# A four-layer graph network: layer 1's message and update products as 2x2 blocks over pairs of graphs

## The chip, the core and the metric

The kernel runs on one core of one Trainium2 chip. The metric is the time of one execution on the device in microseconds (us); lower is better. The engines are called here as in the profile: PE (TensorE, matrix products; PEld is its weight load), DVE (VectorE), ACT (ScalarE), POOL (GpSimd) and SP (SyncE, which only issues DMAs here).

## What is computed

There are 128 graphs of 128 nodes, with 256 features a node, and an integer adjacency matrix for each graph. Four layers follow one another, each inside a residual connection and a layer norm. All numbers are float32.

```
def _L1_gnn_ref(x, adj, W_msg, W_upd, bias):
    a = adj.astype(x.dtype)
    h = jnp.einsum('bnf,fu->bnu', x, W_msg)
    msg_sum = jnp.einsum('bij,biu->bju', a, h)
    deg = jnp.sum(a, axis=1)
    messages = jnp.where(deg[..., None] > 0, msg_sum / jnp.maximum(deg, 1.0)[..., None], 0.0)
    out = jnp.einsum('bnf,fu->bnu', x, W_upd) + messages + bias
    return jax.nn.relu(out)

x = _layernorm(x + _L0_gnn_ref(x, adj, a0, a1, a2, a3), axis=-1)   # four scores by edge type, softmax
x = _layernorm(x + _L1_gnn_ref(x, adj, W_msg, W_upd, bias), axis=-1)
x = _layernorm(x + _L2_gnn_ref(x, adj, weight, w_ih, ...), axis=-1)  # three steps of a gated unit (GRU)
x = _layernorm(x + _L3_gnn_ref(x, adj, W, a), axis=-1)             # attention
```

The change is in layer 1: the two products x W_upd and x W_msg, each 128 nodes x 256 features by 256 x 256, for every graph.

## The kernel before

**Groups.** Four graphs make a group (G = 4), and 32 groups pass through the four layers. The 256 features lie as two chunks of 128 (KC = 2)[...]. The work of several groups is interleaved: while one group is in its GRU, which takes two periods, others are in layers 0, 1 and 3.

**The order.** No engine order is written out by hand. The program first records all operations (`Op`), with what each must wait for, and gives each a nominal time with `paced(start, end)`: the layer's window in units of PERIOD, shifted by the group's number. Then a list scheduler at the end of the file issues them. It keeps for each engine the time at which it becomes free, with assumed costs (`pe_cost`, `dve_cost`, `act_cost`, `pool_cost`), an assumed DMA landing time (LANDING) and assumed hops between engines (HOP and PE_HOP for operations marked urgent, SLACK for the others). Among the operations that are ready by then it takes the one with the least nominal time. The GRU's operations are marked urgent; on all engines but PE they count as EAGER us earlier. The operations that copy an unfinished sum out of PSUM (`snapshot`) count as RUSH us earlier still. The scheduler also hands out buffers, PSUM banks among them. Every engine then runs its list strictly in the order so found, and waits where an operand is not there yet. Operations of POOL and DVE that the program takes to exclude one another are marked with `waits` and `holds`. All recorded calls are issued from one helper, so that every row of the profile has line L232, and rows are told apart by tile names.

**Layer 1** (`layer1`, from line 591). `s.x1T`, written `xT` there, holds the normalised output of layer 0 with features on partitions, [128, graph, chunk, node]. It comes by DMA; for group 0 by transposes on PE and a copy on ACT. `w_um` [128, chunk, 512] holds W_upd in its first 256 columns and W_msg in the rest. For each graph, lines 599 to 607 take a PSUM bank (`bank()`, tag `ps`, four of them; the GRU gates have four more, tag `gate`), add two products of 512 columns into it, one for each chunk, then copy the message half with ACT and add the bias to the update half with DVE, both into `hu`. Column 512 of `hu` is one, so that the product with the adjacency (line 611) gives the degree too. DVE divides, adds, takes the maximum with zero and adds the residual; `normalise` follows, and the result `xb` goes to the GRU.

**The GRU's gates** (`gru`, `sums`, `gate`) already form their products as 2x2 blocks with seven products. Blocks of features and of weights are added and subtracted first (`t_h` by POOL, `t_m` by DVE). Four of the products then accumulate in a bank called `shared`, which is copied out between them, and three go to the bank `other`.

**Layer 3** ends with `ninv`, the negated reciprocal of the softmax sums, four numbers a partition, made by DVE in line 876.

**Transposes** (`turned`, `back`): DVE transposes 32x32 blocks into a tile `z` (four buffers), SP writes it to DRAM and reads it back in block order.

Of the kernel before, what the change touches and what calls it, by code (L numbers as in the profile page):

```python
# [18 lines left out]
def kernel(  # L19
# [39 lines left out]
    B, N, D = x.shape  # L59
# [80 lines left out]
    def bank(tag="ps"):  # L140
        return tile_of(tag, [P, 512], 4, F32, psum)
# [94 lines left out]

    LANDING = 4.2
    HOP = 0.235  # L240
    PE_HOP = 0.55
    SLACK = 0.873

    def pe_cost(op, n, sums):
        return 0.11 if op == "transpose" else 0.222 if n <= P else 0.003 + n / 599.0
# [1 line left out]
    SPLIT = 0.056  # L247

    def dve_cost(op, n, sums):
        return 0.14 + n * (0.00056 if op in FAST else 0.00106)  # L250

    def act_cost(op, n, sums):
        return 0.6 if op == "dma_start" else 0.17 + n * 0.001 + (0.2 if sums else 0.0)
# [9 lines left out]
    engines = (PE, DVE, ACT, POOL, SP)  # L263


    PERIOD = 82.744
    SPAN = 2.0
    EAGER, RUSH = 5.34, 0.516
    L0_START, L0_END, L1_START, L1_END, L3_START, L3_END = -2.032, -1.293, -0.75, -0.05, 0.173, 0.919
    H_END, M_START, M_END = 0.179, 0.179, 0.503  # L270

    def paced(start, end, pe_only=False):

# [18 lines left out]
    neg_half = tile_of("neg_half", [P, G])  # L292
    acol = tile_of("acol", [P, 4, KC])
    w_um = tile_of("w_um", [P, KC, 2 * D])
    bias_row = tile_of("bias_row", [P, D])
    bih = tile_of("bih", [P, NGC])
    bhh = tile_of("bhh", [P, NGC])
# [10 lines left out]
    def weights():  # L308
# [91 lines left out]
        DVE.tensor_add(brz, bih[:, : 2 * KC], bhh[:, : 2 * KC])  # L400
        DVE.tensor_scalar_mul(brz, brz, 0.5)
        DVE.tensor_scalar_mul(bhn, bhh[:, 2 * KC :], 0.5)

        scr = tile_of("t_n", [P, D], 2)
        for c in range(KC):
# [16 lines left out]
    def turned(src, n, tag):  # L422

        way = tile_of(f"way_{tag}", [n, P, P], 8 if tag == "2" else 4, F32, dram)
        for first in range(0, n, G):
            z = tile_of("z", [P, G, P], 4)[:, : min(n, G)]
            DVE.transpose(z, src[:, first : first + G])
            SP.dma_start(out=way[first : first + G].rearrange("n p c -> p n c"), in_=z)
        return way
# [161 lines left out]
    def layer1(g, s):  # L591
        x1, a_f, xT = s.x1, s.a_f, s.x1T

        s.m_gt = tile_of("m_gt", [P, G, N], 3, U8)
        POOL.tensor_scalar(s.m_gt, a_f, 0.0, None, op0=OP.is_gt)
        s.a_ne = tile_of("a_ne", [P, G, N], 3, BF16)
        DVE.tensor_scalar(s.a_ne, a_f, 0.0, None, op0=OP.not_equal)
        hu = []
        for b in range(G):
            hu.append(tile_of("hu", [P, 2 * D + 1], 2))  # L600
            POOL.memset(hu[b][:, 2 * D :], 1.0)
            ps = bank()
            with PE:
                for c in range(KC):
                    PE.matmul(ps, xT[:, b, c, :], w_um[:, c, :], start=(c == 0), stop=(c == KC - 1))
            ACT.copy(hu[b][:, D : 2 * D], ps[:, D:])
            DVE.tensor_add(hu[b][:, :D], ps[:, :D], bias_row)
        res = tile_of("xb", [P, G, D], 2)
        for b in range(G):
            ps = bank()  # L610
            PE.matmul(ps[:, : D + 1], a_f[:, b, :], hu[b][:, D:], start=True, stop=True)
            fac = tile_of("fac", [P, 1], 4)
            DVE.tensor_scalar_max(fac, ps[:, D : D + 1], 1.0)
            DVE.reciprocal(fac, fac)
            DVE.scalar_tensor_tensor(
                fac, ps[:, D : D + 1], 0.0, fac, op0=OP.is_gt, op1=OP.mult
            )
            DVE.scalar_tensor_tensor(
                res[:, b, :], ps[:, :D], fac, hu[b][:, :D], op0=OP.mult, op1=OP.add
            )  # L620
            if b % 2 == 1:
                two = slice(b - 1, b + 1)
                DVE.scalar_tensor_tensor(res[:, two], res[:, two], 0.0, x1[:, two], op0=OP.max, op1=OP.add)
        normalise(res, *statistics(res, "1"), "1", g == 0)

        s.way_x2 = tile_of("way_x2", [P, G, D], 4, F32, dram)
        SP.dma_start(out=s.way_x2, in_=res)
        s.hT, s.parts, s.ways = [], [], []
        for c in range(KC):
            t = tile_of("h0T", [P, T], 4)  # L630
            cols = slice(c * P, (c + 1) * P)
            if g == 0:
                turned_quick(t, [res[:, b, cols] for b in range(G)])
            s.ways.append(turned(res[:, :, cols], G, "2"))
            if g > 0:
                back(t, s.ways[c])
            s.hT.append(t)
        for c in range(KC):
            s.parts.append(split(res[:, :, c * P : (c + 1) * P], POOL))
# [171 lines left out]
    def layer3(g, s, first, last):  # L811


        n = last - first
        end = g == NG - 1
        names = LAST if first else {}
        two, three = ("2b", "3b") if first else ("2", "3")

        def tile(tag, shape, bufs=1):
            tag, bufs = names.get(tag, (tag, bufs))  # L820
            return tile_of(tag, shape, bufs)

        rT = []
        for c in range(KC):
            t = tile("rT", [P, n * N], 2)
            cols = slice(first * N, last * N)
            back(t, s.ways[c][first:last])
            (DVE if end else POOL).tensor_add(t, t, s.hT[c][:, cols])
            rT.append(t)
        x3 = tile("xc", [P, n, D])  # L830
        SP.dma_start(out=x3, in_=s.way_x2[:, first:last])
        for c in range(KC):
            cols = slice(c * P, (c + 1) * P)
            DVE.tensor_add(x3[:, :, cols], x3[:, :, cols], s.hn[c][:, first:last])
        mv, rstd = statistics(x3, two)
        wh = tile("wh", [P, n, 2 + D])
        for b in range(n):
            ps = bank()
            with PE:
                for c in range(KC):  # L840
                    PE.matmul(
                        ps[:, : 2 + D], rT[c][:, b * N : (b + 1) * N], w3x[:, c, :],
                        start=(c == 0), stop=(c == KC - 1),
                    )
            ACT.mul(wh[:, b, :], ps[:, : 2 + D], rstd[:, b : b + 1])


        f = tile("e", [P, 4 * n, 32])
        e = f.rearrange("p (k b) c -> p b k c", [P, n, 4, 32], b=n)
        if end:  # L850
            ps = bank()
            with PE:
                for b in range(n):
                    PE.transpose(ps[:, b * N : (b + 1) * N], wh[:, b, 1:2].to_broadcast([P, N]), ident)
            rows = [ps[:, b * N : (b + 1) * N].rearrange("p (k c) -> p k c", c=32) for b in range(n)]
        else:
            z = tile_of("z_f", [P, 32])
            DVE.transpose(z, wh[:, :, 1:9])
            way = tile_of("way_f", [P, 32], 4, F32, dram)
            SP.dma_start(out=way, in_=z)  # L860
            SP.dma_start(out=f, in_=way.rearrange("(m r) c -> r m c", [8, 16, 32], r=8)[0].partition_broadcast(P))
            rows = [e[:, b] for b in range(n)]
        alpha = tile("alpha3", [P, n, N])
        POOL.memset(alpha, NEG3)
        for b in range(n):
            leaky(e[:, b], rows[b], wh[:, b, 0:1])
        BLOCKS = "p b (k c) -> p b k c"
        DVE.copy_predicated(
            alpha.rearrange(BLOCKS, c=32), s.m_gt[:, first:last].rearrange(BLOCKS, c=32), e
        )  # L870
        pT, rinv = softmax(alpha, three, end, tile)
        normalise(x3, mv, rstd, two, end)

        res = tile("xd", [P, n, D])
        ninv = tile_of(f"ninv_{three}", [P, n], 2)
        DVE.tensor_scalar_mul(ninv, rinv, -1.0)
        for h in range(n // 2):
            ps = bank()
            with PE:
                for j in range(2):  # L880
                    b = 2 * h + j
                    PE.matmul(ps[:, j * D : (j + 1) * D], pT[:, b, :], wh[:, b, 2:], start=True, stop=True)
            for j in range(2):
                b = 2 * h + j
                pb = ps[:, j * D : (j + 1) * D]
                ACT.activation(res[:, b, :], pb, AF.Relu, scale=rinv[:, b : b + 1])
                ACT.activation(pb, pb, AF.Relu, scale=ninv[:, b : b + 1])
            half = slice(2 * h, 2 * h + 2)
            ACT.activation(ps, ps, AF.Exp, scale=-1.0)
            (DVE if end else POOL).tensor_add(res[:, half], res[:, half], x3[:, half])  # L890
            DVE.scalar_tensor_tensor(
                res[:, half], ps.rearrange("p (b d) -> p b d", [P, 2, D], b=2), -1.0, res[:, half],
                op0=OP.add, op1=OP.add,
            )
        normalise(res, *statistics(res, three), three, end)
        SP.dma_start(out=out[g * G + first : g * G + last].rearrange("b n d -> n b d"), in_=res)
# [139 lines left out]
```

## Time and profile before

| | |
|---|---|
| median of 3 runs | 2764.72 us (2764.5 to 2765.69) |
| the profiled execution | 2763.69 us |
| its span, first to last instruction | 2761.8 us |
| mean granted TensorE clock | 0.991 |
| DMA | 321.88 MB, mean 117 GB/s |
| ACT copy hu<-ps, 128x256 | 128 times, mean 368 ns |
| DVE add hu<-ps,bias_row, 128x256 | 128 times, mean 413 ns |
| DVE t_z<-gate,t_z, 128x512 | 96 times, mean 668 ns |
| POOL t_h sums, 128x256 | 384 in four rows, together 323.7 us |
| DVE ninv<-rinv, 128x4 | 31 times, mean 676 ns |

A row of the profile names the engine, the operation, output<-inputs by tile name, the shape and the count; then the busy time in us and the mean of one in ns; then how long the engine was idle just before such instructions, and what ended that. A float32 product leaves two records, so that 512 records of 128x512 on `w_um` are 256 products: 8 for each of 32 groups. The ends of matmuls are modelled and overlap the next start.

### The profile page before, as it was taken

The numbers are of one execution on the slowest core, as the hardware profiler recorded it, in microseconds if no ns is written. First come the engines' busy times: TensorE is split into PE (matmuls) and PEld (weight loads), VectorE is DVE, ScalarE is ACT, GpSimd is POOL, SyncE is SP. The second block draws the span as 40 slices with busy tenths as digits, with TensorE's granted clock in tenths as the row PEclk, the third lists the DMA queues.
The fourth block names the chain that finished last, engine by engine and source line by source line (L and its number), as shares of the span: only waits on it lengthen the run. The fifth ranks groups of instructions, "written<-read, shape, count | busy, mean of one in ns | idle before, by whom it ended". The sixth has DMA issues, their size and how long they took to land.

```text
span 2761.8 us, 44048 instructions
## 1 busy us (share of the span) xinstructions
PE 2702.3 (98%) x13756; PEld 2138.1 (77%) x13756; DVE 2304.1 (83%) x5108; ACT 1584.2 (57%) x3704; POOL 1666.2 (60%) x1606
## 2 busy tenths in 40 slices
PE   8899999999999999999999999999999999999996
PEld 5677787887887887887887887887887887787774
DVE  5787888888888888888888888888888898888875
ACT  4454665555665655665655665655665655665554
POOL 4544666655666655666655666655676655675542
PEclk9999999999999999999999999999999999999996
DMA  5545555555555556555655556655556555545441
GB/s 121 129 90 99 115 126 129 120 109 124 122 125 131 121 108 129 118 124 133 121 107 127 121 121 134 121 110 123 121 121 134 124 109 120 116 110 118 99 88 43
DMA packets 1397130, 321.88 MB, mean 117 GB/s; under 512 B 1142560, under 2 KB 1388448, under 8 KB 1396896
## 3 DMA queue, kind: packets, MB, share of 16 engines
q1 hardware_dynamic: 1394448, 316.69, 53.7%
q10 hardware_dynamic: 2448, 2.36, 0.3%
q8 instruction: 111, 1.82, 0.3%
q14 instruction: 123, 1.01, 0.1%
HBM read 185.74 MB, written 133.15 MB: 115 GB/s over the span
## 4 chain that ended last, share of the span: by engine, by line
PE 94%; DVE 3%; POOL 1%; ACT 1%; DMA 1%; issue 1%; ACTq 0%; POOLq 0%; DVEq 0%; SPq 0%
PE gate L232 52%; PE ps L232 42%; DVE t_r L232 0%; POOL t_h L232 0%; DVE xb L232 0%; DVE st L232 0%; DMA rest<-in_L_gnn_w_hh_dram 0%; DVE z L232 0%; POOL rstd L232 0%; DMA hn<-in_L_gnn_weight_dram 0%; POOL xa L232 0%; DVE xa L232 0%; DVE t_d L232 0%; POOL t_d L232 0%; DVE hT L232 0%
## 5 line engine op out<-in xcount | busy, mean ns | idle before, releaser
L232 ACT ACTIVATE q<-gate,bhn 128x256 f32<-128x256 f32 x384 | 183.0, 477 | 314.4 <-PE gate L232 313.1
L232 PE MATMUL ps<-agT,c_gi 128*128 128x512 f32 x768 | 356.0, 592 | 0.0
L232 PE MATMUL gate<-t_h,w_hhT 128*128 128x256 f32 x1152 | 345.2, 381 | 5.7 <-ACT t_z L232 4.3
L232 PE MATMUL gate<-t_h,w_sh 128*128 128x256 f32 x1152 | 337.1, 383 | 4.2 <-ACT q L232 1.7
L232 POOL TENSOR_TENSOR rstd<-rstd,neg_half 128x4 f32<-128x4 f32 (+1 forms) x128 | 142.4, 1112 | 218.2 <-DVE rstd L232 215.1
L232 PEld LDWEIGHTS gate<-t_h,w_sh 128*128 128x128 f32 x1152 | 213.7, 191 | 62.8 <-issue 30.4
L232 PEld LDWEIGHTS ps<-xs,xT 128*128 128x128 f32 x2048 | 249.7, 193 | 11.5 <-ACT xs L232 2.6
L232 PEld LDWEIGHTS gate<-t_h,w_hhT 128*128 128x128 f32 x1152 | 211.7, 191 | 56.1 <-issue 16.3
L232 PE MATMUL ps<-xs,xT 128*128 128x128 f32 x2048 | 251.8, 276 | 2.2 <-ACT xs L232 1.3
L232 ACT COPY t_z<-gate 128x256 f32<-128x256 f32 x288 | 107.1, 372 | 244.6 <-PE gate L232 244.0
L232 PE MATMUL ps<-w_um,x1T 128*128 128x512 f32 x512 | 237.1, 595 | 0.2 <-ACT x1T L232 0.2
L232 PEld LDWEIGHTS ps<-agT,c_gi 128*128 128x128 f32 x768 | 145.8, 190 | 114.5 <-issue 106.0
L232 PE MATMUL gate<-agT,c_gi 128*128 128x256 f32 x768 | 229.2, 380 | 2.6 <-ACT agT L232 2.6
L232 PE MATMUL gate<-t_m,c_gi 128*128 128x256 f32 x768 | 228.5, 379 | 0.0
L232 PE MATMUL gate<-t_m,w_sm 128*128 128x256 f32 x768 | 228.4, 379 | 0.0
L232 PE MATMUL gate<-hT,w_hhT 128*128 128x256 f32 x768 | 222.8, 385 | 5.6 <-DVE hT L232 5.6
L232 POOL TENSOR_SCALAR mk<-a_f 128x512 uint8<-128x512 f32 x128 | 201.3, 1579 | 12.2 <-DVE alpha L232 6.6
L232 ACT ACTIVATE xs<-xT,acol 128x512 f32<-128x512 f32 x256 | 182.1, 717 | 40.9 <-PE ps L232 31.5
L232 POOL MEMSET hu<- 128x1 f32 x128 | 10.3, 96 | 303.8 <-DVE fac L232 224.5
L232 DVE TENSOR_TENSOR t_z<-gate,t_z 128x256 f32<-128x256 f32 x192 | 104.2, 543 | 101.4 <-ACT t_z L232 53.7
L232 POOL TENSOR_TENSOR t_d<-h0T,t_n 128x512 f32<-128x512 f32 x64 | 82.9, 1295 | 174.0 <-ACT t_n L232 171.1
L232 PEld LDWEIGHTS gate<-hT,w_hhT 128*128 128x128 f32 x768 | 141.8, 191 | 48.1 <-issue 23.6
(197 smaller groups left out, 7280.1 us busy)
## 6 DMA issues: line engine op xcount, KB each, us to landing
way_h<-z SPq DMA_DIRECT2D x190, 256.0 KB, 2.4
hn<-way_h SPq DMA_DIRECT2D x760, 64.0 KB, 2.4
way<-z SPq DMA_DIRECT2D x126, 256.0 KB, 3.2
x_blocks<-in_x_dram SPq DMA_DIRECT2D x256, 64.0 KB, 2.3
x_in<-in_x_dram SPq DMA_DIRECT2D x32, 512.0 KB, 3.8
way_x<-xb SPq DMA_DIRECT2D x32, 512.0 KB, 2.9
way_p<-z SPq DMA_DIRECT2D x62, 256.0 KB, 2.6
probT<-way_p SPq DMA_DIRECT2D x248, 64.0 KB, 2.3
```

The lines of the kernel that those rows point to most:

```text
L232: getattr(self.engine, name)(*[a.real() if isinstance(a, View) else a for a in args], **{k: a.real() if isinstance(a, View) else a for k, ...
```

## The change

Graphs are taken in pairs. Of a pair, x11 and x12 are the two feature chunks of the first graph, x21 and x22 those of the second; of the weights, b11 and b12 are chunk 0 of W_upd and W_msg, b21 and b22 chunk 1. The four 128x256 blocks of results (two graphs, two weights) are now formed from seven products of 256 columns instead of four of 512. Three sums of weights (`w_x`) and the difference that replaces b12 in `w_um` are made once, on POOL. Three sums of features for each pair (`t_x`) and the difference that replaces x21 in `xT` are made by POOL for both pairs of a group at a time. Each pair holds two banks; between the products in `shared` there is one bias addition by DVE and two copies by ACT. Further, `ninv` moves to ACT, `z` has three buffers, and constants of the scheduler have other values.

```diff
-    LANDING = 4.2
+    LANDING = 3.91
     HOP = 0.235
-    PE_HOP = 0.55
-    SLACK = 0.873
+    PE_HOP = 0.478
+    SLACK = 0.61
...
     def dve_cost(op, n, sums):
-        return 0.14 + n * (0.00056 if op in FAST else 0.00106)
+        return 0.095 + n * (0.00056 if op in FAST else 0.00106) + (0.08 if sums else 0.0)
...
-    PERIOD = 82.744
+    PERIOD = 88.831
     SPAN = 2.0
-    EAGER, RUSH = 5.34, 0.516
-    L0_START, L0_END, L1_START, L1_END, L3_START, L3_END = -2.032, -1.293, -0.75, -0.05, 0.173, 0.919
-    H_END, M_START, M_END = 0.179, 0.179, 0.503
+    EAGER, RUSH = 26.109, 4.31
+    L0_START, L0_END, L1_START, L1_END, L3_START, L3_END = -2.032, -1.293, -0.701, -0.122, 0.297, 0.767
+    H_END, M_START, M_END = 0.141, 0.122, 0.7
...
+    w_x = tile_of("w_x", [P, 3, D])
...
+        b11, b12, b21, b22 = [w_um[:, c, n * D : (n + 1) * D] for c in range(KC) for n in range(2)]
+        POOL.tensor_sub(w_x[:, 1], b22, b12)
+        POOL.tensor_sub(b12, b12, b11)
+        POOL.tensor_sub(w_x[:, 0], b22, b12)
+        POOL.tensor_sub(w_x[:, 2], b21, w_x[:, 0])
...
-            z = tile_of("z", [P, G, P], 4)[:, : min(n, G)]
+            z = tile_of("z", [P, G, P], 3)[:, : min(n, G)]
...
+        t = tile_of("t_x", [P, 3, 2, N])
+        x11, x12, x21, x22 = [
+            xT.rearrange("p (h j) c n -> p j c h n", [P, 2, KC, 2, N], j=2)[:, j, c] for j in range(2) for c in range(KC)
+        ]
+        POOL.tensor_add(t[:, 0], x21, x22)
+        POOL.tensor_sub(x21, x11, x21)
+        POOL.tensor_sub(t[:, 1], t[:, 0], x11)
+        POOL.tensor_sub(t[:, 2], x12, t[:, 1])
+        U, M = slice(0, D), slice(D, 2 * D)
         hu = []
-        for b in range(G):
-            hu.append(tile_of("hu", [P, 2 * D + 1], 2))
-            POOL.memset(hu[b][:, 2 * D :], 1.0)
-            ps = bank()
-            with PE:
-                for c in range(KC):
-                    PE.matmul(ps, xT[:, b, c, :], w_um[:, c, :], start=(c == 0), stop=(c == KC - 1))
-            ACT.copy(hu[b][:, D : 2 * D], ps[:, D:])
-            DVE.tensor_add(hu[b][:, :D], ps[:, :D], bias_row)
+        for h in range(G // 2):
+            pair = tile_of("hu", [P, 2, 2 * D + 1], 2)
+            POOL.memset(pair[:, :, 2 * D :], 1.0)
+            hu += [pair[:, 0], pair[:, 1]]
+            shared, other = bank(), bank()
+            first, second = 2 * h, 2 * h + 1
+
+            def add(cols, x, w, start=False, stop=False):
+                PE.matmul(cols, x, w, start=start, stop=stop, skip_group_check=True)
+
+            def snapshot(to):
+                ACT.copy(to, shared[:, :D])
+                ops[-1].rush = RUSH
+
+            add(shared[:, :D], xT[:, first, 0, :], w_um[:, 0, U], True)
+            DVE.tensor_add(pair[:, 0, U], shared[:, :D], bias_row)
+            add(other[:, U], xT[:, first, 1, :], w_um[:, 1, U], True)
+            add(shared[:, :D], t[:, 1, h], w_x[:, 0])
+            snapshot(pair[:, 0, M])
+            add(other[:, M], t[:, 0, h], w_um[:, 0, M])
+            add(shared[:, :D], xT[:, second, 0, :], w_x[:, 1])
+            snapshot(pair[:, 1, M])
+            DVE.tensor_add(pair[:, 1, M], other[:, M], pair[:, 1, M])
+            add(shared[:, :D], xT[:, second, 1, :], w_x[:, 2], stop=True)
+            DVE.tensor_add(pair[:, 1, U], shared[:, :D], bias_row)
+            add(other[:, M], t[:, 2, h], w_um[:, 1, M], stop=True)
+            DVE.tensor_add(pair[:, 0, : 2 * D], other, pair[:, 0, : 2 * D])
...
-        DVE.tensor_scalar_mul(ninv, rinv, -1.0)
+        ACT.mul(ninv, rinv, -1.0)
```

## The prediction

> **What bounds the kernel now.** I read the page's header and busy table first, then its costliest groups, then busy time by stretches of the span, then the waits of TensorE in the middle stretch, then the order in time. From the page:
>
> ```profile
> span 2761.8 us, 44048 instructions
> PE 2702.3 (98%) x13756; PEld 2138.1 (77%) x13756; DVE 2304.1 (83%) x5108; ACT 1584.2 (57%) x3704; POOL 1666.2 (60%) x1606
> ...
> PE 94%; DVE 3%; POOL 1%; ACT 1%; DMA 1%; issue 1%; ACTq 0%; POOLq 0%; DVEq 0%; SPq 0%
> ...
> L232 PE MATMUL ps<-w_um,x1T 128*128 128x512 f32 x512 | 237.1, 595 | 0.2 <-ACT x1T L232 0.2
> ```
>
> TensorE is busy 98% and makes up 94% of the chain that ended last. The last row is the group that the change replaces. The stretches (columns: length, then PE, weight loads, DVE, ACT, POOL) say where the idle 59 us lie:
>
> ```profile
> 0.00:270.00 270.00, 247.99 (x1254) 189.09 (x1255) 192.81 (x437) 125.44 (x282) 130.58 (x143) 0.99 0.52 110
> 270.00:2580.00 2310.00, 2307.17 (x11852) 1839.18 (x11851) 1989.71 (x4411) 1364.58 (x3196) 1457.53 (x1392) 1.00 0.56 120
> 2580.00:2761.80 181.80, 147.16 (x653) 109.86 (x651) 121.56 (x263) 94.17 (x228) 78.08 (x72) 0.88 0.35 78
> ```
>
> In the middle 2310 us TensorE is idle for 3; the rest is start (22) and drain (35). All that TensorE waited for in the middle is this:
>
> ```profile
> PE gate L232 <- ACT agT L232: 1.7, 1, 1.7
> PE gate L232 <- ACT t_z L232: 1.0, 2, 0.6
> ```
>
> So in the middle time is TensorE work, and only TensorE work counts. Busy time hides small gaps, because matmuls overlap in the records. The pitch from start to start, in the timeline, is the true price:
>
> ```profile
> 1000.55 1.88 PE L232 MATMUL ps<-w_um,x1T 128*128 128x512 f32 x4
> ...
> 1006.31 0.59 PE L232 MATMUL gate<-t_h,w_hhT 128*128 128x256 f32 x2
> 1006.74 0.59 PE L232 MATMUL gate<-hT,w_sh 128*128 128x256 f32 x2
> ```
>
> A float32 product is two records. Four records of 512 columns take 1.88 us, the last one 0.59 with its modelled end: (1.88 - 0.59) / 3 = 0.43 us a record, 0.86 a product. A product of 256 columns starts 0.43 after the one before it. Between 1000 and 1160 us I added up such pitches: 155.9 of 159.3 us, so some 2% are gaps that the busy row does not show, 49 us over the middle.
>
> **What the Trainium skill says.** "Perfetto Trace Analysis", section Identifying the Most-Contended Engine: busy time of matmuls is a poor measure, since they are pipelined. The trace agrees: mean record 595 ns, pitch 430. "FP8 and Floating Point Precision", TensorE Precision Notes: true FP32 takes four passes; the trace shows two records a product and a cost proportional to columns (0.86 for 512, 0.43 for 256), all that I use. "TensorE: Matmul & The Clock Gate", Weight-path perf modes: the fast weight load is not for FP32. Here a float32 load takes 190 ns and a bfloat16 one 99. This matters because halving the columns leaves a 190 ns load only 215 ns to hide behind; the 256-column gate products above keep exactly 0.43, so it still hides. "SBUF — State Buffer", Who interferes with whom: a VectorE instruction with two inputs in SBUF, or in a two-port mode, excludes a GpSimd one that reads SBUF for a whole instruction. The trace agrees: the 4-element ninv takes
>
> ```profile
> L232 DVE TENSOR_SCALAR ninv<-rinv x32: 176/665/989, 283.1 to 2750.5; 128x4 f32<-128x4 f32 x31, 128x2 f32<-128x2 f32 x1
> ```
>
> (minimum, median, maximum ns): 0.18 alone, 0.67 with a wait.
>
> **The change part by part.**
>
> *TensorE.* Removed: 8 products of 512 columns a group, 8 x 0.86 = 6.88 us. Added: 2 pairs x 7 products of 256 columns, 14 x 0.43 = 6.02. Saved 0.86 a group, 32 x 0.86 = 27.5 us, nearly all of it in the dense stretch (group 0 lies in the start). Loads rise by 12 records of 0.19, hidden as above.
>
> *Waits inside a pair.* The bank `shared` is read between its four products: one bias add (VectorE) and two snapshots (ScalarE), so three waits a pair, 192 in all, each with one product of 0.43 on `other` between. The GRU gates do the same (3 gates x about 3 waits x 96 steps, some 900). Lower bound 0, if other groups' products are issued in between. Upper bound on what such waits cost a dense stretch: if all 49 unseen us were theirs, 49 / 900 = 0.054 each, 192 x 0.054 = 10 us. I take 4. What one costs with nothing between is on the chain of the drain (start, length):
>
> ```profile
> 2693.78 1.24 PE gate L232 x2
> 2695.02 0.03 issue
> 2695.04 0.48 ACT q L232
> 2695.53 0.04 issue
> 2695.57 1.24 PE gate L232 x2
> ```
>
> 1.79 us a turn against 0.86 of work: 0.9 exposed. Behind a waiting product all of TensorE stands, in order, GRU included.
>
> *VectorE.* Removed: 4 adds of 256 columns from PSUM at 0.413 (row hu<-ps,bias_row) and ninv, 0.68. Added: 6 of those and 2 of 512 at 0.67 (row t_z<-gate,t_z 128x512). Net 8 - 4 instructions, 3.82 - 1.65 - 0.68 = +1.5 us a group. Group starts are 81.1 us apart (first and last w_um products 54.7 and 2569.9, 31 intervals). VectorE has 1989.7 / 2310 = 86%, 69.9 us a group; it goes to 71.4 of 80.3, 89%. Below TensorE, so nothing on the path while order gives slack.
>
> *GpSimd.* Four sums of 256 columns a group. The t_h rows are the same operation: 384 in 324 us, 0.84 each with port waits (0.73 median). 3.4 us a group, 63% to 67-68%. Upper bound on harm: VectorE shut out for all 3.4, then 74.8 of 80.3, 93%: still not the bound. Two one-column memsets go. In the dense stretch the sums have GpSimd's idle third as cover; without it they delay t_h and t_d queued behind, which feed the GRU.
>
> *ScalarE.* Four copies of 256 columns stay four; ninv comes, about 0.2. Nothing.
>
> *Start and drain.* Four weight sums of about 0.73 on GpSimd near 40 us fit before its idle 2.1 at 42.7 and 8.6 at 51.5: 0, at most +3. Group 0: x1T is there at 55.2, GpSimd is idle until 60.1; t[:,1] takes three sums, 2.3 us, while four products (1.7) need none. The chain runs from there through xb to the first GRU: from -2 (pair 0's second graph no longer waits for its own 1.7 us of products) to +4, I take +1. In the drain ninv stands on the chain with 0.89 at 2720.5; on ScalarE it costs 0.2: -0.7.
>
> *Buffers and order.* z goes from 4 to 3: 12 transposes a group (378 over the run), each held some 0.7 + 2.6 us, is half a buffer on average; bursts of two meet three slots, 0. The new weights' and sums' tiles carry no wait. hu becomes pairs, two deep, so four graphs instead of two: nothing lost. A pair holds two of the four `ps` banks for 3 us and longer, where a graph held one for about 2.4; no row shows them short. No DMA is added, and SP's queue keeps its items. The constants (assumed hops, PERIOD, EAGER, RUSH, windows) change the order of everything. No row prices that. Bounds: half of the unseen gaps won back, -24; a fiftieth of the dense stretch lost, +46. I take 0.
>
> Sum: -27.5 + 4 + 1 - 0.7 = -23.2. The profiled execution took 2763.69 (span 2761.8 and 1.9 around it): 2740.5. The median of the runs, 2764.72, is 1.0 above it, so 2741.5; I say 2741.
>
> **The rivals.**
> *More than that:* order closes half of the unseen gaps: 2741 - 24 = 2717. For: the gaps are there. Against: they are spread over all kinds of neighbours.
> *Half given back:* VectorE near 90-93% and the port lock make it late for bias adds and gate sums, 0.4 us a group lost on TensorE: 2741 + 13 = 2754. For: VectorE is the second engine. Against: it has 300 us idle in the middle.
> *No change:* all of 0.75 a group is lost: 2765.
> *Slower:* the 192 new waits are exposed, because order now assumes shorter delays (SLACK 0.61 for 0.873, PE_HOP 0.478 for 0.55) than VectorE and ScalarE keep for layer 1, whose operations stand behind the GRU's by EAGER 26. At a quarter of 0.9, 0.23 a wait: 2741 - 4 + 192 x 0.23 = 2781. It decides the sign from (27.5 - 0.3) / 192 = 0.14 us a wait. Against: some 900 such waits cost almost nothing now.
> That the change doesn't do what it says: writing the blocks out, the seven products give both halves of both graphs; the count is 14 a group. No weight on it.
>
> **How the numbers follow.** Forecast 0.57 (own range 2733 to 2749), more 0.10, half 0.13, none 0.05, slower 0.15. 0.2% is 5.5 us, about what a measurement of this kernel tells from no change. Faster by over that: 0.57 + 0.10 + most of half = 0.78; within 0.07; slower 0.15. The range leaves out the lower half of "more" and more than half of "slower", and holds the unknown order in part: 2722 to 2772.
>
> **What would show it.** Right: 448 products (896 records) of 128x256 on w_um, w_x with t_x and x1T, at pitch 0.43; TensorE idle in the middle still under 10 us; group starts 80.3 apart; POOL up by 100 us, DVE by 50 to 100. Wrong: waits of ps on hu (ACT or DVE) of tens of us, or pitch sums falling below 97% of the middle; then the exposed waits or the order have eaten it. A drain longer than 182 us by over 10 would also upset it.

## The result

The changed kernel takes 2802.36 us (median of 4 runs, 2801.59 to 2803.68) against 2764.76 before: a ratio of 1.0136, 95% interval 1.0118 to 1.0153, 38 us slower. From the page of the changed kernel, in the order in which the lines of before were shown:

```profile
span 2801.9 us, 44966 instructions
PE 2702.4 (96%) x14140; PEld 2210.9 (79%) x14140; DVE 2313.4 (83%) x5203; ACT 1603.0 (57%) x3737; POOL 1821.3 (65%) x1674
...
PE 70%; DVE 14%; POOL 9%; issue 2%; DMA 2%; ACT 2%; SPq 1%; ACTq 0%; DVEq 0%; POOLq 0%
```

TensorE's busy time is what it was, in a span that is 40 us longer, and the chain that ended last now runs 14% through VectorE and 9% through GpSimd, where it ran 94% on TensorE. The stretches (length, then PE, weight loads, DVE, ACT, POOL):

```profile
0.00:270.00 270.00, 245.44 (x1280) 197.59 (x1281) 193.25 (x449) 122.18 (x270) 143.61 (x154) 0.97 0.51 106
270.00:2580.00 2310.00, 2274.63 (x12053) 1874.50 (x12052) 1970.62 (x4427) 1370.28 (x3200) 1588.59 (x1440) 1.00 0.57 120
2580.00:2801.90 221.90, 182.35 (x811) 138.81 (x809) 149.51 (x329) 110.58 (x269) 89.08 (x81) 0.89 0.35 75
```

What TensorE waited for in the middle stretch (who waited for whom, us in total, times, longest):

```profile
PE gate L232 <- POOL t_h L232: 26.6, 25, 1.3
PE gate L232 <- DMA x1T<-way: 4.5, 4, 1.3
PE gate L232 <- ACT t_z L232: 1.2, 3, 0.5
```

In the middle stretch TensorE was idle for 3 us and is now idle for 35. The last list says for what: for t_h, the sums that GpSimd makes for the GRU's gates. The four entries put down to the DMA of x1T stand before the same product, one period from their neighbours in the timeline, so they are the same wait.

A period is the time from one start of `a_f` (the adjacency made float, on GpSimd, once a group) to the next, in the median of the last 25. The first and the last of these starts, before and then after:

```profile
353.65 0.61 POOL L232 CAST a_f<-adj_in 128x512 f32<-128x512 int32 x1
2420.46 0.91 POOL L232 CAST a_f<-adj_in 128x512 f32<-128x512 int32 x1
...
359.87 0.61 POOL L232 CAST a_f<-adj_in 128x512 f32<-128x512 int32 x1
2452.57 0.61 POOL L232 CAST a_f<-adj_in 128x512 f32<-128x512 int32 x1
```

The period was 82.67 us; it is 83.70. The starts of the products in one period, less their pitches, give gaps of 0.46 us before and 2.32 after, so that TensorE's work is 82.2 before and 81.4 after. The products save about what they should, 0.83 us a group, and the gaps take 1.86. The period's larger gap on TensorE is the last row here (start, length, then idle time before):

```profile
1040.78 0.60 PE L232 MATMUL gate<-t_h,w_hhT 128*128 128x256 f32 x2
...
1043.67 0.59 PE L232 MATMUL gate<-agT,w_sm 128*128 128x256 f32 x2
1045.32 0.70 PE L232 MATMUL gate<-t_h,w_hhT 128*128 128x256 f32 x2 [1.06 <-DMA x1T<-way]
```

The product after 1043.67 should start at 1044.10; it starts at 1045.32, 1.22 late. The period's other large gap, 0.38, lies inside the score block of layer 0 that ends at 1040.78. At the same time GpSimd does this:

```profile
1037.54 1.04 POOL L232 TENSOR_TENSOR rstd<-rstd,neg_half 128x4 f32<-128x4 f32 x1
1038.68 2.96 POOL L232 TENSOR_SCALAR xb<-xb,mv,rstd 128x256 f32<-128x256 f32 x2
1041.62 2.01 POOL L232 TENSOR_SCALAR mk<-a_f 128x512 uint8<-128x512 f32 x1
1043.58 0.10 POOL L232 MEMSET hu<- 128x2 f32 x1
1043.62 0.52 POOL L232 MEMSET alpha<- 128x512 f32 x1
1044.11 1.85 POOL L232 TENSOR_TENSOR t_h<-hT 128x256 f32<-128x256 f32 x2
1045.92 1.53 POOL L232 TENSOR_TENSOR t_h<-hT,t_h 128x256 f32<-128x256 f32 x2
```

There is one buffer t_h. Its last reader is the product at 1040.78, done about 1041.4. From then on the next sums could run, and TensorE needs the first at 1044.1. But a mask for a later score block (mk, 2.01) and two memsets stand ahead in GpSimd's queue.

The profiled span grew by 40.0 us: by 6.2 up to the earlier start of each pair above, by 25.9 in the 25 periods between, and by 7.9 after the later one. So about a third of the loss lies in the start and the drain.

### The profile page after: what moved, and what is told of

Same layout as the page of the kernel before. It is cut to its first block, busy times and chain, and to the rows that moved or that the text cites. A ratio compares the mean times of both kernels' runs of the same rounds, so it can differ in the third digit from the quotient of the medians.

```text
span 2801.9 us, 44966 instructions
## 1 busy us (share of the span) xinstructions
PE 2702.4 (96%) x14140; PEld 2210.9 (79%) x14140; DVE 2313.4 (83%) x5203; ACT 1603.0 (57%) x3737; POOL 1821.3 (65%) x1674
## 4 chain that ended last, share of the span: by engine, by line
PE 70%; DVE 14%; POOL 9%; issue 2%; DMA 2%; ACT 2%; SPq 1%; ACTq 0%; DVEq 0%; POOLq 0%
PE gate L232 37%; PE ps L232 32%; POOL xb L232 3%; DVE t_r L232 2%; DVE z L232 2%; POOL mk L232 2%; DVE xb L232 2%; POOL rstd L232 1%; POOL t_h L232 1%; DVE st L232 1%; SPq L232 1%; DVE hT L232 1%; POOL xa L232 1%; DVE t_m L232 1%; DVE q L232 1%
## 5 line engine op out<-in xcount | busy, mean ns | idle before, releaser
L232 PE MATMUL gate<-t_h,w_sh 128*128 128x256 f32 x1152 | 348.1, 385 | 9.1 <-ACT q L232 3.2
L232 PE MATMUL ps<-xs,xT 128*128 128x128 f32 x2048 | 262.1, 280 | 4.9 <-ACT xs L232 0.8
L232 POOL TENSOR_TENSOR t_d<-hT,t_n 128x512 f32<-128x512 f32 x128 | 162.5, 1279 | 85.7 <-ACT t_n L232 82.8
L232 DVE SCALAR_TENSOR_TENSOR t_r<-t_r,q 128x512 f32<-128x512 f32 x192 | 132.6, 691 | 80.8 <-ACT t_r L232 80.8
L232 ACT ACTIVATE t_r<-t_r,brz 128x256 f32<-128x256 f32 x192 | 118.2, 615 | 129.2 <-DVE t_r L232 129.2
L232 ACT COPY t_r<-gate 128x256 f32<-128x256 f32 x288 | 106.4, 369 | 147.4 <-PE gate L232 142.3
```

Source lines behind the costliest of these rows:

```text
L232: getattr(self.engine, name)(*[a.real() if isinstance(a, View) else a for a in args], **{k: a.real() if isinstance(a, View) else a for k, ...
```

## The experiments

Two theories were set against each other. Theory O: the order that the scheduler builds with the new constants makes GpSimd's gate sums late. Theory S: the four feature sums that the change gives to GpSimd push them back. For the edits of an order the scheduler ran as before, its list of operations was kept and edited, and the list was then issued. Each result below is the median, then the ratio to the kernel before with its 95% interval.

**The constants alone, and the rest alone.** The first kernel is before with

```diff
-    LANDING = 4.2
+    LANDING = 3.91
...
-    PERIOD = 82.744
+    PERIOD = 88.831
...
-    EAGER, RUSH = 5.34, 0.516
+    EAGER, RUSH = 26.109, 4.31
```

and the other constants of the change; the second is the changed kernel with the constants of before.

> The kernel before with nothing but the changed kernel's scheduler constants and DVE cost formula (eight products, bias and copies, four z buffers and ninv as before). Theory O (the order that the new constants give puts GpSimd's gate sums too late, and TensorE waits for them): slower than before by 30 to 60 us, 2795 to 2825, with one or two waits a period of TensorE for t_h. Theory S (the four feature sums added on GpSimd push the gate sums back): within 8 us of before, 2757 to 2773.

> The changed kernel with the constants and DVE cost formula of before. Theory O: the saved 26 us of products come through, 2735 to 2750. Theory S: GpSimd still carries the sums, so TensorE still waits for t_h once or twice a period: 2775 or more.

Measured: 2843.93 us, 1.0288 (1.0271 to 1.0305), and 2856.11 us, 1.0333 (1.0318 to 1.0349). The first has the sign that Theory O forecast, but lies above its range: the new constants alone slow the kernel of before by 80 us, and TensorE waits for t_h with no feature sum on GpSimd. That wait is only one among several, 11 us in the middle stretch:

```profile
PE ps L232 <- DVE rest L232: 13.0, 16, 0.9
PE gate L232 <- POOL t_h L232: 11.1, 8, 1.4
PE gate L232 <- DVE q L232: 9.1, 19, 0.7
```

But the old constants did not bring the saving out either. The second time lies in the range of Theory S, without the cause that S names: TensorE waited 1.0 us for t_h in the middle stretch, and for other things far more:

```profile
PE gate L232 <- ACT t_z L232: 16.6, 16, 2.9
PE gate L232 <- DVE t_z L232: 16.4, 19, 4.4
```

So neither set of constants is good or bad by itself. Each pair of program and constants is another order, and these four lie up to 91 us apart. To compare parts, the order has to be held.

**The gate sums first.** On GpSimd only, what stands directly ahead of the sums goes behind them (the issued list, in short):

```diff
 POOL xb (2x)
-POOL mk; memset hu; memset alpha
 POOL t_h (4x)
+POOL mk; memset hu; memset alpha
```

> The changed kernel with the same order on TensorE, but on GpSimd the mask mk and the memsets that stand directly ahead of a quartet of gate sums t_h are issued after it. Theory O: the 1.2 us gap of each period ahead of gate<-t_h goes, 28 of them, 30 to 35 us: 2767 to 2773; the 0.4 us gap in the scores stays. Theory S: GpSimd as a whole is late, the gap comes back at another product: over 2790.

Measured: 2776.02 us (2771.26 to 2780.5), 1.0043 (1.0028 to 1.0058): just above the forecast. Of the 38 us 26 are back from this one move; the profiled execution, at a span of 2769.5, has 32 back. In the timeline of GpSimd

```profile
1027.39 2.95 POOL L232 TENSOR_SCALAR xb<-xb,mv,rstd 128x256 f32<-128x256 f32 x2
1030.31 1.93 POOL L232 TENSOR_TENSOR t_h<-hT 128x256 f32<-128x256 f32 x2
1032.20 1.86 POOL L232 TENSOR_TENSOR t_h<-hT,t_h 128x256 f32<-128x256 f32 x2
1034.04 1.51 POOL L232 TENSOR_SCALAR mk<-a_f 128x512 uint8<-128x512 f32 x1
```

the sums start as xb ends, and the period is 82.37 with gaps of 1.0. The wait for t_h in the middle falls from 26.6 us to 2.3. The period is now 0.30 shorter than before the change: in the middle the saving begins to show, and what is still lost lies in the start and the drain (table below).

**The feature sums on VectorE, and left out.** First the four lines `POOL.tensor_add(t[:, 0], x21, x22)` and so on as `DVE.`, scheduled anew; then the changed kernel's order with those four operations not issued.

> The changed kernel with the four feature sums of layer 1 on VectorE, so that GpSimd carries what it did before; the scheduler makes a new order with the same constants. Theory S: 30 us or more better than the changed kernel, 2740 to 2770. Theory O: the constants still decide, within 20 us of 2802.

> The changed kernel, every engine in the same order, but the four feature sums of each group on GpSimd are not issued: the seven products read a constant tile in place of t_x and the unchanged x21, so that layer 1's messages are not the reference's. Theory S (the sums push the gate sums back): the 1.2 us gap ahead of gate<-t_h goes, 30 us or more: below 2775. Theory O (what stands directly ahead of the gate sums, after the old t_h is released, is what makes them late; the feature sums run where GpSimd has slack): within 6 us of 2802, 2796 to 2806, the gap still 1.2 us.

Measured: 2909.65 us, 1.0528 (1.0513 to 1.0544), and 2803.97 us, 1.0145 (1.013 to 1.016). The first is a new order again and fits neither theory; it says nothing on the sums. The second holds the order, and it decides: without a single feature sum the time is that of the changed kernel, as Theory O forecast, and so is the wait:

```profile
PE gate L232 <- POOL t_h L232: 26.8, 25, 1.3
PE gate L232 <- DMA x1T<-way: 3.2, 3, 1.1
```

Theory S falls. GpSimd's 93 us of feature sums run where it has time.

**Shorter work ahead of the sums.** Every order as in the changed kernel, but

```diff
-res[:, b, :]                 # normalisation xb on POOL, 256 columns
+res[:, b, : D // 2]
```

> The changed kernel with every order unchanged; on GpSimd the two normalisations xb of layer 1 that stand ahead of the mask and the gate sums work on 128 of their 256 columns, so that half of each even graph's features goes on without normalisation. Theory O, in the form that GpSimd's operations ahead of the gate sums last longer (xb 2.96 us for two) than the scheduler's formula gives them (0.2 + 256 x 0.00266 = 0.88 each): the gap of 1.2 us ahead of gate<-t_h goes without any move, 2765 to 2775. Rival R (the gate sums wait for the release of the single t_h buffer, so that they start no earlier, whatever is ahead of them): within 8 us of 2802.

Measured: 2765.69 us (2764.04 to 2769.04, 20 runs), 1.0007 (1.0 to 1.0014): all but 1 us of the 38 are back. With mask and memsets still ahead of the sums the gap is gone:

```profile
1026.23 2.20 POOL L232 TENSOR_SCALAR xb<-xb,mv,rstd 128x128 f32<-128x128 f32 x2
1028.40 1.74 POOL L232 TENSOR_SCALAR mk<-a_f 128x512 uint8<-128x512 f32 x1
1030.09 0.10 POOL L232 MEMSET hu<- 128x2 f32 x1
1030.12 0.52 POOL L232 MEMSET alpha<- 128x512 f32 x1
1030.61 1.42 POOL L232 TENSOR_TENSOR t_h<-hT 128x256 f32<-128x256 f32 x2
```

The time is in the range of Theory O, and Rival R falls. About a microsecond of GpSimd's time ahead of the sums made this gap: xb and mk together take 3.94 us here, 4.97 in the changed kernel. The scheduler's formula for these operations gives 2 x 0.88 for xb, 1.56 for mk, 2 x 0.55 for the memsets and 2 x 0.84 for the first two sums, 6.10 us; from 1038.68 to 1045.96 they took 7.28. The difference, 1.18, has the size of the gap. That the formula is why the scheduler chose this order is not shown: the kernel before uses the same formula and has no such gap, and the formula with measured durations, below, left gaps too, some of them at t_h.

**The second gap.** As gate_sums_first, and on TensorE (in short)

```diff
-scores; gate<-t_h,w_hhT; gate<-t_m,c_gi
+gate<-t_h,w_hhT; gate<-t_m,c_gi; scores
```

> As gate_sums_first, and in each period the second of two score blocks of layer 0 that stand 0.86 us apart on TensorE is issued one pair of gate products later. Theory O: the 0.39 us gap inside that block goes too, 27 of them, 10 us below gate_sums_first: 2761 to 2768. Rival: the gap moves to the next products, no difference.

Measured: 2780.58 us, 1.006 (1.0043 to 1.0077), a miss for Theory O; the rival, that the gap moves, was right. The gap of 0.39 went, and one of 0.76 came ahead of the next product of the gate:

```profile
PE gate L232 <- ACT t_z L232: 17.2, 30, 0.6
```

The score block had been what TensorE did while ScalarE copied out the `shared` bank; moved, it left that wait bare.

**TensorE's work alone.** Before, with every order, wait and buffer, but

```diff
-PE.matmul(ps, xT[:, b, 1, :], w_um[:, 1, :])   # the second of each two
+PE.matmul(ps[:, :384], xT[:, b, 1, :], w_um[:, 1, :384])
```

> The kernel before with every order, wait and buffer unchanged, but of each pair of 512-column products in layer 1 the second covers 384 columns, 7/8 of the products' columns as in the change; the last 128 message features lack half of their sum. Theory P (TensorE work saved in an order that keeps it fed is time saved, one for one): 128 x 128 columns at 0.215 us per 128, 27 us: 2735 to 2741. Rival Q (another engine or the cycle of waits between the GRU steps is as long as TensorE's work, so that the saving turns into gaps): 2750 or more.

Measured: 2735.96 us (2735.53 to 2736.78), 0.9897 (0.9881 to 0.9914), 28 us less. The middle is as full as before, and the period is 81.82, 0.85 less:

```profile
270.00:2580.00 2310.00, 2305.32 (x11965) 1855.97 (x11964) 2009.13 (x4450) 1376.93 (x3231) 1478.77 (x1410) 1.00 0.57 122
```

So in this order, which keeps TensorE fed, work saved is time saved, one for one. It is the saving in columns that this shows, not the seven products themselves.

**Other orders for the seven products.** Three tries to find an order that shows the saving: two sets of constants with GpSimd's measured durations in the cost formula, and one in which each operation's priority is the time that before's order gave it.

> The changed kernel with other scheduler constants, and GpSimd's costs as measured (two-scalar operations of up to 256 columns 1.3 us instead of 0.88, of 512 columns 1.65, memsets 0.1 plus 0.00085 a column, sums of 256 columns 0.89); the seven products, the feature sums on GpSimd and the three z buffers stay. Theory O: with an order built on GpSimd's real durations the gaps of 1.2 and 0.4 us a period go and the saved products show: 2745 to 2765, at or below before. Rival: seven products can't be scheduled without such gaps, since ScalarE's and GpSimd's answers are needed more often: 2775 or more.

> As seven_products_new_order_a with another set of constants (EAGER 51 instead of 28, PERIOD 83.7 instead of 95.6, shorter assumed hops). Theory O: 2745 to 2775. Rival: 2775 or more.

> The seven products, feature sums on GpSimd, paired hu and three z buffers of the change (ninv on VectorE as before), but each operation's priority in the scheduler is the time at which the kernel before planned it; the operations of layer 1 take the times of those that they replace, the feature sums 8 us ahead, and the assumed costs are those of the change. Theory P (the saving is there for an order that keeps TensorE fed): below before, 2735 to 2760. Rival Q (with seven products layer 1's three waits a pair and the paired banks break that order, and gaps of a microsecond a period come back): 2765 to 2800.

Measured: 2797.23 us, 1.0119 (1.0104 to 1.0134); 2823.21 us, 1.0216 (1.0199 to 1.0233); 2821.72 us, 1.0207 (1.0193 to 1.0221). All three miss the theory's range. The first two lie in the rival's, the third above both. Each has waits of its own that come back every period (middle stretch, the three runs in turn):

```profile
PE gate L232 <- POOL t_h L232: 11.4, 27, 0.4
PE gate L232 <- ACT t_z L232: 9.0, 28, 0.7
...
PE gate L232 <- ACT q L232: 30.9, 26, 1.2
...
PE gate L235 <- DVE t_z L235: 47.0, 25, 2.4
```

In the last one the timeline of VectorE, with two rows of GpSimd, is this:

```profile
1048.73 1.28 POOL L235 TENSOR_TENSOR t_d<-hT,t_n 128x512 f32<-128x512 f32 x1
1048.85 1.19 DVE L235 TENSOR_SCALAR rstd<-mv 128x4 f32<-128x4 f32 x1
1049.96 1.30 DVE L235 SCALAR_TENSOR_TENSOR t_r<-t_r,q 128x512 f32<-128x512 f32 x1
1049.97 1.86 POOL L235 TENSOR_TENSOR t_h<-hT 128x256 f32<-128x256 f32 x2
1051.29 0.69 DVE L235 TENSOR_TENSOR t_r<-t_r,ps 128x512 f32<-128x512 f32 x1
1051.89 0.65 DVE L235 TENSOR_SCALAR ninv<-rinv 128x4 f32<-128x4 f32 x1
1052.46 0.41 DVE L235 TENSOR_TENSOR t_z<-gate,t_z 128x256 f32<-128x256 f32 x1
```

TensorE stood 2.40 us for that t_z. Four operations ahead of it took 3.8 us. At 1044.56 such an rstd had run 0.17, and at 1044.64 such a t_r 0.68.

No version with the seven products was found that beats the kernel before; the best that does all the work is gate_sums_first at 2776. That none can is not shown. Where each version spends its time, from the starts of `a_f` in the profiled executions (us):

| | up to the first of the last 26 starts | 25 periods | after the last start |
|---|---|---|---|
| before | 353.7 | 2066.8 | 341.4 |
| changed | 359.9 | 2092.7 | 349.3 |
| changed, feature sums left out | 360.9 | 2092.3 | 349.2 |
| gate sums first | 359.1 | 2060.6 | 349.7 |
| shorter xb | 357.7 | 2059.7 | 348.6 |
| before, new constants | 360.7 | 2126.3 | 360.3 |
| changed, priorities of before | 358.2 | 2121.8 | 340.0 |

With the gate sums first the 25 periods take 6 us less than before, and the start and the drain 14 more. The feature sums are not the reason: with them left out of the changed kernel, both are as long as in it. The drain goes with the order rather than with the seven products: it is 340 with the priorities of before, and 360 in the kernel before with the new constants. The start is 4 us or more longer in every other row than in the first; no run shows why.

## Why the prediction was wrong

The step that failed is the term for the order, put at nothing: "The constants (assumed hops, PERIOD, EAGER, RUSH, windows) change the order of everything. No row prices that. ... I take 0." Its bound for a loss, 46 us, covered the middle stretch only, and the range did not take in even that. Measured, in the 25 periods the gaps grew by 47 us (25 x 1.86) against 21 of saved work (25 x 0.83). Start and drain grew by 14 us together, though some 6 of work should have gone there (an estimate: the other 7 groups at 0.83); that makes about 67 us of gaps against 27 of work, and 40 of span. In the 25 periods about 31 us of gaps lie ahead of one gate product and 10 in one score block. That GpSimd's queue ahead of the gate sums makes the first is shown from two sides: the sums moved ahead, and shorter work ahead of them. The cause of the score block's gap and of the longer start, and the place in the order that lengthens the drain, stay open. It also stays open which of the constants matters, and how much of the new order is due to them and how much to the new operations: exchanging either gave another order altogether.

- Saved work: 0.86 us a group and 27.5 in all predicted; 0.83 a group after, and 28 us for the same columns with the order of before. Right.
- The waits inside a pair: 4 us predicted. No wait of TensorE for hu is in the list of the middle stretch. The term was rather too large.
- "All 49 unseen us": wrong. Between 1000 and 1160 us the starts and pitches leave about 1 us of gaps, not 3.4. A period before has 0.46, the 25 periods 11. The order before had almost no gaps to win back, and the rival that went faster by closing them had no ground.
- "Group starts are 81.1 us apart": this mean takes in the first and last groups, which follow one another more closely. In the middle they are 82.67 apart before and 83.70 after, so the sign "80.3 apart" started from the wrong figure. The sum of the forecast did not use it.
- GpSimd: the feature sums were put at 0.84 each and took 0.73, and "they delay t_h" was named for the case without cover. They had cover. What delayed t_h was not added but stood elsewhere in the order. GpSimd's busy time grew by 155 us, where 100 were forecast: 96 are the sums of features and weights, and the rest is that its other operations lasted longer in sum (`rest<-rest` 68 us before, 90 after).
- VectorE: +48 us predicted, +9 measured. The added operations took 70 (hu<-ps,hu) and ninv's 21 went, as predicted, but other operations lasted 40 less in sum (`t_d<-t_z,t_d` 177 us before, 153 after). VectorE's operations shortened and GpSimd's lengthened, which fits waits between the two that changed sides; no run tested it.
- ninv: 0.205 us on ScalarE for 0.676 on VectorE, as predicted.
- Buffers and DMA: no wait for `ps` banks or for a free z stands among the waits of TensorE and VectorE in the middle stretch. The step from four z to three was not tried apart.
- The slower rival had the right sign and blamed the order, but its place was wrong: layer 1's 192 new waits cost nothing that shows in the middle stretch, and one wait a period of the GRU, whose operations the change does not touch, cost 31 us. Whether the shorter assumed delays are to blame, as it said, was not tested apart from the other constants.

## What to carry to other kernels

When one engine is 100% busy in a stretch and the order was built for it, price a change of the order apart from the change of the work: here the work was worth -28 us and all the rest, mostly gaps of the new order, +66 by difference. To learn what an edit is worth, hold the order of every engine and change one thing; the kernels that were scheduled anew here measured mostly their new order. In a periodic pipeline look at one period: where the engine that sets the time has no slack, an operation that comes 1.2 us late in each period costs 1.2 us times the number of periods, whichever engine is at fault. Then look at the start and the drain too, which no period shows.

## What the runs showed of the hardware

An operation's duration varied with what ran beside it. In the changed kernel xb on GpSimd took 1.21 us at the least for 256 columns and 1.48 in the mean. In the last run above a VectorE operation that had taken 0.68 took 1.30 beside GpSimd's t_h, and one that had taken 0.17 took 1.19 beside its t_d. The Trainium skill, "SBUF — State Buffer", section Who interferes with whom, says that a VectorE operation with two SBUF inputs contends with a GpSimd operation that reads SBUF, and that one in a two-port mode and a GpSimd operation block each other for a whole instruction; these numbers fit that, though no run tested it alone. In this kernel a 128x256 float32 product kept its pitch of 0.43 us with a weight load of 190 ns for each of its two records, and the measured saving of 0.83 us a group against 0.86 by pitch leaves little that splitting 512 columns in two could have cost on TensorE.
